# A four-layer graph network on one core: new first and last batches, relu of centred rows on ScalarE, identity transposes where TensorE would rest

## The chip, the cores and the metric

The kernel runs on one core of a Trainium2 chip. The metric is the device time of one execution in microseconds, median of several runs. A core has TensorE (PE, matmuls into eight PSUM banks), VectorE (DVE), ScalarE (ACT), GpSimd (POOL) and SyncE (SP, which issues DMA). All data is fp32, except two masks in bf16.

## The reference

Thirty-two graphs (batches) of 512 nodes with 128 features go through four layers. All share one sparse, symmetric adjacency matrix of 512 x 512. Each layer adds its result to x; before each, x is normalized over features and passed through relu.

```python
h = relu(layernorm(x)); x = x + gcn(h)        # layer 0
# A_hat = adj + I; d = rowsum(A_hat) ** -0.5
# gcn(h) = (d[:, None] * A_hat * d[None, :]) @ h @ W.T + b
h = relu(layernorm(x)); x = x + ggnn(h)       # layer 1, five steps:
# m = adj @ h
# z = sigmoid([m, m] @ w3.T + h @ u3.T + ...);  r = sigmoid([m, m] @ w4.T + h @ u3.T + ...)
# hv = tanh([m, m] @ w5.T + (r * h) @ u5.T + ...);  h = (1 - z) * h + z * hv
h = relu(layernorm(x)); x = x + elu(gat(h))   # layer 2
h = relu(layernorm(x)); x = x + gat(h)        # layer 3
# gat: g = h @ W; e = leaky_relu(src[:, None] + dst[None, :]); masked softmax over neighbours; @ g
```

The exponential of a leaky relu of a sum is a maximum of two products, so the kernel takes exponentials of three columns only, a maximum, and a product with the mask.

## The kernel before

Every operation is recorded with an engine, an estimated cost and a due time. A small list scheduler (`Plan`) simulates the engines and emits the instructions in the order it finds; it tries several parameter pairs and keeps the one with the earliest simulated end. Buffers (`bank` are the eight PSUM banks) are handed out by the plan too. On the chip each engine runs its own list in order and waits for semaphores.

Batches go in pairs. Two batches share the seven block products of a Strassen-like scheme (`products`, line L516 in the profile); batches 0 to 3 use plain products in layer 0 (`product`, L551):

```python
def product(h, mT, due):                              # L551
    p, m = Val("bank"), Val("m")
    for c in range(C):                                # C = 4, MM = 0.858
        op("PE", MM, due, lambda c=c: nc.tensor.matmul(flat(p.t), chunk(h, c), mT.t[:, c, :], start=(c == 0), stop=(c == C - 1)),
           r=[h[c], mT[c]], w=[p, m])
    op("ACT", A, due, lambda: nc.scalar.copy(flat(m.t), flat(p.t)), r=[p], w=[m])
    return m
```

At the start the adjacency is loaded, turned on TensorE (L285) and summed on VectorE (L288). GpSimd makes d by a power, TensorE spreads d over a row (L300), and VectorE makes the normalized matrix anT (L308, L311), which the first product of layer 0 needs. Weights are turned on TensorE (L364). The masks of layers 2 and 3 are made soon after (L340).

A gate step of layer 1 is three groups of matmuls (L603 to L618), three tanh and four VectorE operations. Its new state must be turned for the next step. This is done by DMA ("shuttle"), except in the last steps, where TensorE turns it (L448):

```python
if due >= STEPS * B - EASE:                           # EASE = 0
    p = to_features(new, due + 2, *([] if last else [h]))   # 4 transposes on TensorE
    [...]
```

The attention of the last four batches (`near`) does everything without DMA, since nothing is left to hide it:

```python
def norm(b, y, due):
    # norm_stats: 4 bn_stats (L406), 4 bn_aggr (L410), ve = var + eps (L411), rstd = ve ** -0.5 on GpSimd (L413)
    mv, rstd = norm_stats(b, due)
    for c in range(C):                                # L432
        op("DVE", 0.16, due, lambda c=c: nc.vector.tensor_scalar(
            y.t[:, c, :], xb.t[:, c, :], mv.t[:, c, 0:1], rstd.t[:, c:c + 1], op0=ALU.subtract, op1=ALU.mult), ...)
[...]
if near:
    norm(b, y, due)
    pT = to_features(y, due + 1, gT)                  # L448
    op("ACT", A, due + 1, lambda: nc.scalar.activation(gT..., pT..., AF.Relu), r=[pT], w=[gT])   # L663
[...]                                                 # heads: 4 matmuls of gT with w_aug (L678)
    # exp of three columns of each half (L680); g scaled by one of them (L685)
    spread()                                          # 4 transposes of a column into a bank (L698)
    op("ACT", A, due + 2, lambda: nc.scalar.copy(row..., pr...), r=[pr], w=[row, e])             # L700
for j in range(C):                                    # L713
    op("DVE", 0.68, due + 3, lambda j=j: nc.vector.scalar_tensor_tensor(
        e.t[:, j, :], row.t, h.t[:, j, D + 1:D + 2], maskT[l].t[:, j, :], op0=ALU.max, op1=ALU.mult), ...)
[...]                                                 # mix: 16 matmuls of e with g (L722; L733 for other batches)
```

Then come a reciprocal (L736), for layer 2 the product, exponential and elu (L738, L748 to L752), for layer 3 the last sum (L744) and the output DMA (L755). The near chain of a pass is thus: statistics, power, norm, turn, relu, heads, exponentials, spread, copy, e, mix, finish.

Of the kernel before, what the change touches and what calls it, by code (L numbers as in the profile page):

```python
# [15 lines left out]
P = 128  # L16
EPS = 1e-5
STEPS = 5
# [4 lines left out]
EASE = 0  # L23
FAR0, FAR1 = 2, 4
LANES = 6
# [13 lines left out]
class Op:  # L39
    def __init__(self, engine, cost, due, emit, delay):  # L40
        self.engine, self.cost, self.due, self.emit, self.delay = engine, cost, due, emit, delay
        self.waits, self.then, self.vals = 0, [], []


class Plan:
# [5 lines left out]
    def __init__(self, buffers, ends):  # L51
        self.buffers, self.ends, self.ops = buffers, ends, []

# [41 lines left out]
    def attempt(self, uses, last, hurry):  # L95
# [15 lines left out]
        now, count = 0.0, 0  # L111
# [6 lines left out]
        def start(e):  # L118
            if busy[e]:
                return  # L120
            kept = []
            while ready[e]:
# [4 lines left out]
                if not short:  # L127
                    for v in opens:
                        v.t = free[v.kind].pop()
                    busy[e] = True  # L130
                    o.at = now
                    order.append(o)
                    post(now + o.cost, 0, o)
                    post(now + o.cost + o.delay, 1, o)
                    break
                kept.append(key)
            for key in kept:
                heapq.heappush(ready[e], key)

# [9 lines left out]
        while events:  # L149
            now, _, kind, o = heapq.heappop(events)  # L150
            if kind == 0:
                busy[o.engine] = False
                settle(o, True)
            else:
                done += 1
# [12 lines left out]
def gnn_stack(ctx: ExitStack, tc: tile.TileContext, a: dict, out: bass.AP):  # L168
# [48 lines left out]
    }, [(last, hurry) for last in (170, 173, 176, 179) for hurry in (0.06, 0.08, 0.1, 0.12)])  # L217
# [15 lines left out]
    def load(name, shape, src, due, queue="SP", cost=0.45, delay=2.4):  # L233
# [7 lines left out]
    warm = fixed([P, 1], "warm")  # L241
    op("POOL", 0.8, -1000, lambda: make_identity(nc, ident.t), w=[ident])
    op("POOL", 0.1, -999, lambda: nc.gpsimd.memset(mhalf.t, -0.5), w=[mhalf])
    op("DVE", 0.1, -1000, lambda: nc.vector.memset(warm.t, 0.0), w=[warm])
    op("ACT", 1.4, -1000, lambda: nc.scalar.activation(warm.t, warm.t, AF.Tanh), w=[warm])

    adj_sb = Val("e", C)
    for c in range(C):
        e, q = (("SP", nc.sync), ("ACT", nc.scalar))[c % 2]
        op(e, 0.45, -1001, lambda c=c, q=q: q.dma_start(adj_sb.t[:, c, :], adj[c * P:(c + 1) * P, :]),  # L250
           w=[adj_sb[c]], delay=3.6)
    xs = []
    for b in range(B):
        v = Val("x", C)
        op("SP", 0.95, max(-995 + b, STEPS * b - 20) if b >= 8 else -995 + b, lambda v=v, b=b: nc.sync.dma_start(v.t, x[b].rearrange("(c p) d -> p c d", p=P)),
           w=[v], delay=3)
        xs.append(v)
    w0 = load("w0", [P, D], a["L0_gnn_W"], -993.5)
# [10 lines left out]
    for l, w in ((2, "L2_gnn_W"), (3, "L3_gnn_w")):  # L269
        w_aug[l] = fixed([P, D + 3], f"w_aug{l}", 2)  # L270
        op("SP", 0.45, -990.5, lambda l=l, w=w: nc.sync.dma_start(w_aug[l].t[:, :D], a[w]), w=[w_aug[l][0]], delay=2.4)
# [7 lines left out]
    deg, dinv = fixed(SMALL, "deg", C), fixed(SMALL, "dinv")  # L279
    for c in range(C):  # L280
        p = Val("bank")

        def turn_adj(c=c, p=p):
# [4 lines left out]
        op("DVE", 0.66, -801, lambda c=c: nc.vector.reduce_sum(deg.t[:, c:c + 1], adj_sb.t[:, c, :], axis=mybir.AxisListType.X),  # L288
           r=[adj_sb[c]], w=[deg[c]])
    op("DVE", 0.1, -799, lambda: nc.vector.tensor_scalar_add(deg.t, deg.t, 1.0), w=[deg])  # L290
    op("POOL", 1.0, -1000, lambda: nc.gpsimd.tensor_tensor(dinv.t, deg.t, mhalf.t, ALU.pow), r=[deg, mhalf], w=[dinv])


    anT = fixed([P, C, N], "anT", C)
    drow = Val("bank")
    dinv2 = fixed(SMALL, "dinv2")

    def turn_dinv():
        for c in range(C):
            nc.tensor.transpose(drow.t[:, c, :], dinv.t[:, c:c + 1].to_broadcast([P, P]), ident.t)  # L300
    op("PE", C * TURN, -798, turn_dinv, r=[dinv, ident], w=[drow])
    op("DVE", 0.1, -798, lambda: nc.vector.tensor_mul(dinv2.t, dinv.t, dinv.t), r=[dinv], w=[dinv2])
# [3 lines left out]

    for m in range(C):
        op("DVE", 0.7, -797, lambda m=m: nc.vector.scalar_tensor_tensor(  # L308
            anT.t[:, m, :], adjT.t[:, m, :], dinv.t[:, m:m + 1], flat(drow.t), op0=ALU.mult, op1=ALU.mult),
           r=[adjT, dinv, drow], w=[anT[m]])  # L310
        op("DVE", 0.26, -797, lambda m=m: nc.vector.scalar_tensor_tensor(  # L311
            block(anT.t, m), ident.t, dinv2.t[:, m:m + 1], block(anT.t, m), op0=ALU.mult, op1=ALU.add),
           r=[ident, dinv2], w=[anT[m]])
# [15 lines left out]
    of_adj, of_an = right_factors(adjT, -3), right_factors(anT, 5)  # L329


    maskT = {l: fixed([P, Q, N], f"maskT{l}", C, dtype=BF16) for l in (2, 3)}
    for l in (2, 3):
        far = Val(None, C)
        far.t = tiles(1, [Q, W, C, N], f"far_mask{l}", dram, BF16)[0]
        for c in range(C):
            part = Val("mask", 1)

            def edges(l=l, c=c, part=part):
                nc.vector.tensor_scalar(part.t, adjT.t[:, c, :], 0.0, None, op0=ALU.is_gt)  # L340
                if l == 2:
                    nc.vector.scalar_tensor_tensor(part.t[:, c * P:(c + 1) * P], block(adjT.t, c), -1.0, ident.t,
                                                   op0=ALU.mult, op1=ALU.is_lt)
            op("DVE", 0.35 if l == 3 else 0.6, 4 + l, edges, r=[adjT, ident], w=[part])
            op("SP", 0.4, 4 + l, lambda c=c, far=far, part=part: nc.sync.dma_start(
                far.t[:, :, c, :].rearrange("q i n -> (q i) n"), part.t), r=[part], w=[far[c]], delay=2.2)
        for c in range(C):
            op("SP", 0.4, 4 + l, lambda l=l, c=c, far=far: nc.sync.dma_start(
                maskT[l].t[c * W:(c + 1) * W], far.t[:, :, c, :].rearrange("q i n -> i q n")),
               r=[far], w=[maskT[l][c]], delay=2.2)  # L350
# [6 lines left out]
    def transposed(due, *group):  # L357
# [3 lines left out]
        for i, (parts, _) in enumerate(group):  # L361
# [3 lines left out]
            op("PE", len(parts) * MM1, due, turns, r=[ident, minus] + [q[0] for q in parts], w=[p[i]])  # L365
# [13 lines left out]
    w0T = transposed(-750, (one(w0), 1))  # L379
    gates = transposed(-700, (halves("w4"), 1), (one(raw["u3"]), 1), (halves("w3") + halves("w4", minus), 1), (halves("w5"), 1))  # L380
    u5T = transposed(-690, (one(raw["u5"]), 0.5))
    gats = transposed(-10, (one(w_aug[2]), 1), (one(w_aug[3]), 1))
# [9 lines left out]
    for i, l in enumerate((2, 3)):  # L392
        p = Val("bank")
        op("PE", 0.3, -9, lambda i=i, l=l, p=p: nc.tensor.matmul(p.t[:, 0, :2], gats.t[:, i, :], a_pair[l].t, start=True, stop=True),
# [5 lines left out]
        op("DVE", 0.3, -9, columns, r=[p], w=[w_aug[l][1]])  # L400
# [15 lines left out]
    def norm_relu(b, y, due):  # L416

        xb, off = xs[b], Val("off")
        mv, rstd = norm_stats(b, due)
        op("DVE", 0.1, due, lambda: nc.vector.scalar_tensor_tensor(off.t, mv.t[:, :, 0], -1.0, rstd.t, op0=ALU.mult, op1=ALU.mult),  # L420
# [6 lines left out]
    def norm(b, y, due):  # L427
# [3 lines left out]
        for c in range(C):  # L431
            op("DVE", 0.16, due, lambda c=c: nc.vector.tensor_scalar(  # L432
                y.t[:, c, :], xb.t[:, c, :], mv.t[:, c, 0:1], rstd.t[:, c:c + 1], op0=ALU.subtract, op1=ALU.mult),
               r=[xb[c], mv, rstd], w=[y[c]])

# [111 lines left out]
    def product(h, mT, due):  # L547

        p, m = Val("bank"), Val("m")
        for c in range(C):  # L550
            op("PE", MM, due, lambda c=c: nc.tensor.matmul(flat(p.t), chunk(h, c), mT.t[:, c, :], start=(c == 0), stop=(c == C - 1)),  # L551
               r=[h[c], mT[c]], w=[p, m])
        op("ACT", A, due, lambda: nc.scalar.copy(flat(m.t), flat(p.t)), r=[p], w=[m])
        return m


# [239 lines left out]
```

The softmax here doesn't subtract the row's maximum and nothing guards it: scores larger than these inputs give would overflow.

## Time and profile before

| | us |
|---|---|
| median of 3 runs (1642.45 to 1643.86) | 1642.52 |
| span of the profiled execution | 1643.0 |
| TensorE busy (7250 instructions) | 1617.2 |
| VectorE busy | 1378.8 |
| ScalarE busy | 715.6 |
| GpSimd busy | 144.0 |
| DMA: 159.80 MB, mean | 97 GB/s |

How to read the profile: busy time is the union of an engine's instructions. The profile counts every fp32 matmul as two records and a transpose as one. The ends of matmuls are modelled and overlap, so the distance from one start to the next says more than a duration. The chain goes back from the last instruction: at each step to what released it, or to the instruction before it on its engine. A wait line reads "engine, line <- engine, line that released it: us in total, times, longest".

### The profile page before, as it was taken

The page shows a single profiled execution, that of the slowest core. Times are in us where ns is not written, and L with a number is a line of the kernel's source. Part 1 is how long each engine was busy: PE and PEld are TensorE (multiplying, and loading weights), DVE is VectorE, ACT ScalarE, POOL GpSimd, SP SyncE. Part 2 cuts the span into 40 slices and gives each one's busy share as a digit, 9 for nine tenths or more (in the row PEclk, how much of TensorE's full clock was granted, in tenths as well). Part 3 has the DMA queues.
Part 4 walks back from the last instruction along what each step waited for, and adds up shares of the span by engine and source line. Part 5 has one row for each costly group of instructions (what it writes and reads, how often), then busy time and mean ns, then how long its engine had stood idle before and what let it go on. Part 6 is the DMA issues. An engine that isn't in the chain of part 4 may idle for free.

```text
span 1643.0 us, 23716 instructions
## 1 busy us (share of the span) xinstructions
PE 1617.2 (98%) x7250; PEld 1163.2 (71%) x7250; DVE 1378.8 (84%) x3937; ACT 715.6 (44%) x1573; POOL 144.0 (9%) x136
## 2 busy tenths in 40 slices
PE   8999999999999999999999999999999999999997
PEld 5666567776776777776776767767767777766787
DVE  7977588988888898888888888898887888787897
ACT  4643353535345353343535245343443535343442
POOL 2200000010001111010101001111000000000100
PEclk9999999999999999999999999999999999999999
DMA  5433253543435344353443535344363433424100
GB/s 148 110 74 72 54 123 97 122 103 100 113 84 142 79 110 101 91 141 93 110 113 84 129 90 134 98 105 107 87 139 75 104 76 83 126 72 110 39 27 26
DMA packets 380639, 159.80 MB, mean 97 GB/s; under 512 B 206080, under 2 KB 362080, under 8 KB 380512
## 3 DMA queue, kind: packets, MB, share of 16 engines
q1 hardware_dynamic: 380224, 157.77, 39.3%
q8 instruction: 57, 0.93, 0.2%
q14 instruction: 70, 0.57, 0.1%
q10 hardware_dynamic: 288, 0.52, 0.1%
HBM read 87.30 MB, written 70.89 MB: 96 GB/s over the span
## 4 chain that ended last, share of the span: by engine, by line
PE 94%; DVE 4%; DMA 1%; SPq 0%; issue 0%; ACT 0%; DVEq 0%
PE bank L516 33%; PE bank L733 12%; PE bank L617 8%; PE bank L618 8%; PE bank L610 8%; PE bank L603 8%; PE bank L604 8%; PE bank L678 3%; PE bank L722 2%; PE bank L572 1%; DVE st L406 1%; PE bank L448 1%; DVE S L504 0%; DVE m L529 0%; DMA e<-in_adj_dram 0%
## 5 line engine op out<-in xcount | busy, mean ns | idle before, releaser
L516 PE MATMUL bank<-made,S 128*128 128x256 f32 x1128 | 273.2, 380 | 4.1 <-DVE m L529 3.2
L413 POOL TENSOR_TENSOR rstd<-ve,mhalf 128x4 f32<-128x4 f32 x128 | 142.2, 1113 | 1469.8 <-DVE ve L411 1209.0
L516 PEld LDWEIGHTS bank<-made,S 128*128 128x128 f32 x1128 | 217.2, 196 | 43.3 <-issue 15.6
L521 ACT COPY half<-bank 128x256 f32<-128x256 f32 x282 | 104.7, 371 | 261.9 <-PE bank L516 257.7
L733 PEld LDWEIGHTS bank<-h_gat,e 128*128 128x128 f32 x1792 | 207.3, 192 | 12.8 <-issue 10.0
L733 PE MATMUL bank<-h_gat,e 128*128 128x129 f32 x1792 | 208.5, 275 | 0.2 <-DVE e L713 0.2
L606 ACT ACTIVATE r<-bank,gate_bw 128x512 f32<-128x512 f32 x160 | 109.5, 684 | 196.7 <-PE bank L604 180.2
L622 DVE TENSOR_TENSOR hv<-hv,hT 128x512 f32<-128x512 f32 x160 | 109.7, 686 | 87.4 <-ACT hv L620 86.6
L713 DVE SCALAR_TENSOR_TENSOR e<-row,h_gat,maskT 128x512 f32<-128x512 f32 x256 | 182.7, 741 | 0.0
L608 DVE SCALAR_TENSOR_TENSOR rh<-r,hT 128x512 f32<-128x512 f32 x160 | 109.8, 686 | 77.1 <-ACT r L606 74.3
L617 PE MATMUL bank<-m,wT 128*128 128x512 f32 x320 | 163.5, 592 | 0.0
L603 PE MATMUL bank<-m,wT 128*128 128x512 f32 x320 | 163.4, 592 | 0.0
L618 PE MATMUL bank<-rh,wT 128*128 128x512 f32 x320 | 163.4, 592 | 0.0
L604 PE MATMUL bank<-hT,wT 128*128 128x512 f32 x320 | 163.4, 592 | 0.0
L610 PE MATMUL bank<-m,wT 128*128 128x512 f32 x320 | 163.2, 592 | 0.0
L620 ACT ACTIVATE hv<-bank,gate_bw 128x512 f32<-128x512 f32 x160 | 109.6, 685 | 118.5 <-PE bank L618 117.0
L516 PE MATMUL bank<-adjT,h 128*128 128x256 f32 x640 | 160.6, 380 | 0.4 <-ACT h L423 0.3
L516 PEld LDWEIGHTS bank<-adjT,h 128*128 128x128 f32 x640 | 122.7, 196 | 26.4 <-issue 14.1
L529 DVE TENSOR_TENSOR m<-half,bank 128x256 f32<-128x256 f32 x282 | 115.6, 411 | 25.7 <-PE bank L516 13.7
L612 ACT ACTIVATE z<-bank,gate_bw 128x512 f32<-128x512 f32 x160 | 109.4, 685 | 58.7 <-PE bank L610 54.5
L406 DVE BATCH_NORM_STATS2 st<-x 128x6 f32<-128x128 f32 x512 | 122.4, 277 | 3.6 <-DMA x<-in_x_dram 3.3
L618 PEld LDWEIGHTS bank<-rh,wT 128*128 128x128 f32 x320 | 60.8, 190 | 76.5 <-issue 67.2
(115 smaller groups left out, 2218.2 us busy)
## 6 DMA issues: line engine op xcount, KB each, us to landing
far<-sq SPq DMA_DIRECT2D x936, 64.0 KB
h<-far SPq DMA_DIRECT2D x248, 128.0 KB
gT<-far SPq DMA_DIRECT2D x56, 256.0 KB
row<-line SPq DMA_DIRECT2D x56, 256.0 KB
x<-in_x_dram SPq DMA_DIRECT2D x32, 256.0 KB
out_dram<-x SPq DMA_DIRECT2D x32, 256.0 KB
h<-far SPq DMA_DIRECT2D x28, 256.0 KB
hT<-far SPq DMA_DIRECT2D x104, 64.0 KB
```

What stands on the lines that cost most here:

```text
L406: op("DVE", 0.21, due, lambda c=c: nc.vector.bn_stats(st.t[:, c, :], xb.t[:, c, :]), r=[xb[c]], w=[st[c]])
L413: op("POOL", 1.0, due, lambda: nc.gpsimd.tensor_tensor(rstd.t, ve.t, mhalf.t, ALU.pow), r=[ve, mhalf], w=[rstd])
L516: nc.tensor.matmul(low(r), u[:, l, :], factors[k][0]()[:, l, :], start=fresh and l == 0, stop=l == 1, skip_group_check=not fresh)
L529: op("DVE", HV, due - 5, lambda: nc.vector.tensor_add(out(), u.t, low(t)), r=[u, t], w=[o])
L603: nc.tensor.matmul(flat(gate.t), gates.t[:, 0, :], flat(m.t), start=True, stop=False)
L604: nc.tensor.matmul(flat(gate.t), gates.t[:, 1, :], flat(hT.t), start=False, stop=True)
L608: op("DVE", V, due - 5, lambda: nc.vector.scalar_tensor_tensor(flat(rh.t), flat(r.t), 1.0, flat(hT.t), op0=ALU.add, op1=ALU.mult), r=[r, h ...
L610: op("PE", MM, due + 0.3, lambda: nc.tensor.matmul(flat(gate.t), gates.t[:, 2, :], flat(m.t), start=False, stop=True, skip_group_check=Tru ...
L617: nc.tensor.matmul(flat(cand.t), gates.t[:, 3, :], flat(m.t), start=True, stop=False)
L618: nc.tensor.matmul(flat(cand.t), u5T.t[:, 0, :], flat(rh.t), start=False, stop=True)
L713: op("DVE", 0.68, due + 3, lambda j=j: nc.vector.scalar_tensor_tensor(e.t[:, j, :], row.t, h.t[:, j, D + 1:D + 2], maskT[l].t[:, j, :], op ...
L733: nc.tensor.matmul(pt()[:, c, :D + 1], e.t[:, j, i * P:(i + 1) * P], h.t[:, j, :D + 1], start=(j == 0), stop=(j == C - 1))
```

## The change

It leaves the middle of the computation as it is and redoes both ends:

- *Start.* x of batch 0 is loaded before the adjacency. TensorE runs eight matmuls on a cleared tile while nothing has landed. Layer 0 of batches 0 to 3 multiplies with adjT itself (and a small tile for the blocks on the diagonal with the identity added); d is put into the normalized input and into the last sum instead. So the first product needs neither anT nor the spread of d; these are made after the second product. Two of the four degree sums go to ScalarE. The masks are made later. `begin(b + 2)` records layer 0 of the next pair before layer 1 of this one.
- *Early steps.* The state of the steps with due below 8 (four of them) is turned on TensorE.
- *Near attention.* Since relu(r * (x - mean)) = r * relu(x - mean) for positive r, ScalarE makes relu(x - mean) at once. r goes into the exponentials as a scale and into one small product. The row is read by VectorE from PSUM and not copied; masks in the order this needs are put into anT's memory, which is free by then. Elu and output go in halves.
- *Where the plan leaves TensorE idle.* From 1420 us of the plan's time, if TensorE has rested 0.9 us of the last 3.4 of that time, the plan adds a transpose of the identity into a free bank. Nobody reads it. It is there to hold TensorE's clock.
- Other parameter pairs for the plan.

The core of the diff, with cuts marked `[...]`:

```diff
-EASE = 0
+EARLY = 8
+IDLE_FROM = 1420
+RUN_UP = 8
[...]
+        def keep_going():
+            since = now - self.SPAN                          # 3.4
[...]
+            rest = self.SPAN - sum(min(b, now) - max(a, since) for a, b in work if a < now)
+            if rest < self.REST:                             # 0.9
[...]
+            v = Val("bank")
+            v.t, v.uses = free["bank"].pop(0), 1
+            o = Op("PE", self.IDLE, 0, lambda: self.idle(v), 0)
[...]
-    }, [(last, hurry) for last in (170, 173, 176, 179) for hurry in (0.06, 0.08, 0.1, 0.12)])
+    }, [(171, 0.05), (173, 0.04), (175, 0.07), (176, 0.1), (179, 0.14)],
+        IDLE_FROM, lambda v: nc.tensor.transpose(v.t[:, 0, :], ident.t, ident.t))
[...]
+    def turn_nothing():
+        for _ in range(RUN_UP):
+            nc.tensor.matmul(run_up.t[:, 0, :], warm.t[:, 0, :], warm.t[:, 0, :], start=True, stop=True)
+    op("PE", 0.43 * RUN_UP, -1002, turn_nothing, r=[warm], w=[run_up])
[...]
+        if c < 2:
+            op("ACT", 0.7, -801, lambda c=c, junk=junk: nc.scalar.activation(
+                flat(junk.t), adj_sb.t[:, c, :], AF.Copy, accum_out=deg.t[:, c:c + 1]), ...)
[...]
+    def center_relu(b, y, due):
+        for a in range(2):
[...]                                          # bn_stats and bn_aggr of two row blocks, off = -mean
+            for c in (2 * a, 2 * a + 1):
+                op("ACT", 0.385, due, lambda c=c: nc.scalar.activation(
+                    y.t[:, c, :], xb.t[:, c, :], AF.Relu, bias=off.t[:, c:c + 1]), r=[xb[c], off[a]], w=[y[c]])
+        op("DVE", 0.1, due, lambda: nc.vector.tensor_scalar_add(ve.t, mv.t[:, :, 1], EPS), r=[mv], w=[ve])
+        op("POOL", 1.0, due, lambda: nc.gpsimd.tensor_tensor(rstd.t, ve.t, mhalf.t, ALU.pow), r=[ve, mhalf], w=[rstd])
[...]
-    def product(h, mT, due):
+    def product(h, due):
[...]
+            def times(c=c):
+                for lo, hi in ((0, c), (c, c + 1), (c + 1, C)):
+                    if lo < hi:
+                        right = diag.t[:, c, :] if lo == c else adjT.t[:, c, lo * P:hi * P]
+                        nc.tensor.matmul(flat(p.t)[:, lo * P:hi * P], h.t[:, c, :], right, ...)
[...]
-        if due >= STEPS * B - EASE:
+        if not EARLY <= due < STEPS * B:
[...]
         if near:
-            norm(b, y, due)
+            rstd, g = center_relu(b, y, due), Val("off", 2)
             pT = to_features(y, due + 1, gT)
-            op("ACT", A, due + 1, lambda: nc.scalar.activation(... AF.Relu), r=[pT], w=[gT])
+            op("ACT", A, due + 1, lambda: nc.scalar.copy(flat(gT.t), flat(pT.t)), r=[pT], w=[gT])
[...]
+                    for c in range(2):
+                        nc.scalar.activation(ht()[:, c, D:D + 3], qt()[:, c, D:D + 3], AF.Exp,
+                                             scale=rstd.t[:, 2 * a + c:2 * a + c + 1])
+                op("DVE", 0.08, due + 1, lambda a=a, ht=ht: nc.vector.tensor_mul(
+                    g.t[:, 2 * a:2 * a + 2], ht()[:, :, D], rstd.t[:, 2 * a:2 * a + 2]), ...)
[...]
-            op("ACT", A, due + 2, lambda: nc.scalar.copy(row..., pr...), r=[pr], w=[row, e])
+            row, rows, masked, mask = pr, flat, kept[0], lambda j: kept[1](l, j)
```

## The prediction, made before the changed kernel ran

> **What bounds the kernel now.** I read the page first: the busy time of each engine, the slices and the chain that ended last.
>
> ```profile
> PE 1617.2 (98%) x7250; PEld 1163.2 (71%) x7250; DVE 1378.8 (84%) x3937; ACT 715.6 (44%) x1573; POOL 144.0 (9%) x136
> PE   8999999999999999999999999999999999999997
> PE 94%; DVE 4%; DMA 1%; SPq 0%; issue 0%; ACT 0%; DVEq 0%
> ```
>
> TensorE is busy in 98% of the span and holds 94% of the chain. Nothing outside TensorE can give much, except where it waits. So I made a ledger of the span: the work that TensorE must do, and the rest. For the work I need the distance from one matmul to the next, not its duration (these overlap). The chain in order of time gives it, from runs of one kind:
>
> ```profile
> 201.28 8.63 PE bank L516 x40
> 248.63 3.57 PE bank L733 x32
> 1585.70 0.86 PE bank L610 x2
> 1586.56 0.44 PE bank L448 x4
> ```
>
> The columns are start, length, and what. So a record with 256 columns takes 8.63/40 = 0.216 us, one with 129 takes 0.112, one with 512 takes 0.43, one transpose 0.11. (Each fp32 matmul is two records, each transpose one.) The groups kept apart by shape count 2632 records of 256 columns, 1632 of 512, 2048 of 129, 512 of 131, and 422 of 128 with the transposes: 2632 x 0.216 + 1632 x 0.429 + 2560 x 0.112 + 422 x 0.111 = 568 + 700 + 287 + 47 = 1602 us. The span is 1643.0. TensorE's first record starts at 5.0 us and its last ends at 1638.0, 5.0 before the end. That leaves 1643 - 1602 - 10 = 31 us in which TensorE waits or is slow. The table by stage says where:
>
> ```profile
> 0.00:15.00 15.00, 8.46 (x44) 7.82 (x45) 7.60 (x28) 6.55 (x14) 2.79 (x9) 1.00 0.76 210
> 15.00:50.00 35.00, 33.74 (x121) 19.62 (x120) 33.55 (x146) 21.22 (x50) 9.77 (x9) 1.00 0.45 126
> 50.00:100.00 50.00, 48.94 (x193) 34.88 (x192) 44.97 (x165) 24.22 (x55) 9.70 (x9) 1.00 0.43 91
> 100.00:1450.00 1350.00, 1346.88 (x5906) 963.09 (x5905) 1136.76 (x3165) 590.18 (x1278) 106.97 (x96) 1.00 0.42 101
> 1450.00:1586.50 136.50, 134.09 (x634) 94.84 (x633) 110.40 (x292) 54.96 (x124) 8.75 (x8) 1.00 0.27 69
> 1586.50:1612.00 25.50, 24.57 (x213) 23.61 (x212) 25.00 (x81) 9.72 (x27) 3.50 (x3) 1.00 0.04 11
> 1612.00:1630.00 18.00, 13.10 (x87) 12.19 (x85) 12.75 (x48) 8.07 (x24) 2.52 (x2) 0.81 0.05 16
> 1630.00:1643.00 13.00, 7.38 (x64) 7.22 (x64) 7.72 (x20) 0.67 (x3) 0.00 (x0) 0.97 0.21 61
> ```
>
> The columns are the stage, its length, then busy time of PE, PEld, DVE, ACT and POOL, the granted clock, and DMA. In the 1350 us of the middle TensorE is idle for 3.1 us. In the first 100 it is idle for 6.5 + 1.3 + 1.1 = 8.9, of which 5.0 are the landing of the adjacency. From 1586.5, just after the last gate matmul, it is idle for 0.9 + 4.9 + 5.6 = 11.4, and the clock falls to 0.81 in one stage. The change can only win at the two ends. The chain of the end shows the second one:
>
> ```profile
> 1617.97 0.17 DVE ve L411
> ...
> 1618.53 0.76 DVE e L713
> 1619.29 0.04 issue
> 1619.33 3.81 PE bank L722 x16
> 1623.14 1.71 PE bank L448 x8
> ```
>
> Sixteen L722 records cost 3.81 us there, against 16 x 0.112 = 1.79 elsewhere; eight transposes 1.71 against 0.88. TensorE stood still for 3.2 us before it (the waits list "PE bank L722 <- DVE e L713: 4.3, 2, 3.2"), and ran at half speed after.
>
> **What the Trainium skill says.** "TensorE: Matmul & The Clock Gate", Part 1, says that the array runs at half rate until it has been busy for a window of about 3.4 us, and falls back after an idle one. The trace agrees: at the start 16 transposes took 3.65 us (0.228 each, twice 0.11), and the end is as above. Part 4 of that page says that a transpose does not count as busy in the same way; nothing in the trace before settles this, and it is the doubtful point of the change's identity transposes. "ScalarE: Activation LUTs", What ACT_TABLE_LOAD costs, says that each [128,1] operand of an activation adds about 93 ns. The trace has 482 ns for the relu with bias and scale, so my estimate for the new one with bias alone is 390 ns. "VectorE: DVE Perf Modes", The TRN2 errata, gives an operation that reads PSUM a larger fixed cost than one that reads SBUF (120 against 58 cycles). The trace does not show it: anT<-adjT,dinv,bank reads PSUM and takes 741 ns, e<-row,h_gat,maskT reads SBUF and takes 744. So I take 0.74 us for the new e too.
>
> **The change, part by part.**
>
> *TensorE's own work.* I counted matmuls in the order of instructions of both kernels. Four steps of the first pair (due below 8) now turn their state on TensorE instead of by DMA: 16 transposes x 0.11 = +1.8 us. The products of batches 0 to 3 are cut into 40 matmuls instead of 16, with the same columns: by the fixed part of about 3 ns in each distance above, +0.2. The 29 identity transposes (3.2 us) and the 8 warm-up matmuls (16 records) lie where TensorE has nothing else. Sum: **+2 us**.
>
> *The start.* Before, the first product starts at 14.1 us. By the work ahead of it (16 transposes, 22 weight records and 4 transposes of dinv: 42 x 0.11 = 4.6) it could start at 5.0 + 4.6 = 9.6. The 4.5 us between are the cold clock (16 x 0.12 = 1.9 on the transposes, about 1.2 on the first ten weight records) and the wait of 1.6 for anT. After: the warm-up matmuls begin at about 1.2 us on a cleared tile, so the clock should rise at 5 to 8 instead of about 10: saves 1.5 to 2. The first product reads adjT and a diagonal tile and no longer needs anT nor dinv's transposes: saves 1.6 + 0.4. It needs the scaled y of batch 0, whose chain is the degrees (2 on ScalarE, 2 on VectorE, 0.7 each), the power (1.0) and four multiplies (0.25 each): adjacency at about 5 + 1.5 + 0.2 + 1.1 + 0.4 for the first piece, near 8.5, earlier than the weights, which come by DMA to about 10. Against it, x of batch 0 is loaded ahead of the adjacency: 256 KB more before it, at the stage's 210 GB/s up to +1 us, in part hidden. Between 15 and 100 TensorE waits 2.3 us (copies of m, L516 behind L529, VectorE 96% busy from 15 to 50). Moving the masks, anT and half of the degrees off VectorE's first 50 us should give back some 1.5. Sum: -1.8 - 2.0 - 1.5 + 0.3 = **-5 us**.
>
> *The end, one near pass* (norm, turn, heads, row, e, mix). Before, the chain holds ve 0.17, the power on GpSimd 1.0 and four norms 1.1 between the statistics and the transposes. After, the relu follows the means of each half directly, 4 x 0.29 + 0.1 = 1.3 us on ScalarE (step of 0.385 less 0.093), and the power goes beside the transposes and heads: -1.0. The row is no longer copied from PSUM: -0.59 and a hand-over, together -0.65. More exponentials (four instead of two) and the small multiply for g (0.15): +0.2. So -1.45 a pass, and layers 2 and 3 of the last pair follow each other: -2.9. Elu and output in halves let statistics start on the first half: about -0.7. If the clock stays up: -(3.81 - 1.79) - (1.71 - 0.88) = -2.8, less 0.4 for identity transposes in the way of real work. VectorE: five of the passes lie after 1586.5 (20 norms of L432); each loses 4 x 0.256 and gains 4 small operations of 0.08, -0.7, so -3.5 in all of 45.5 busy us; that shortens queues, and I take -1 of it as path. Sum: **-7 us**.
>
> *The middle.* The scheduler orders all anew with other parameters. Before, it leaves 3.1 + 2.4 us idle from 100 to 1586; I take no change, with a spread of 3.
>
> Total: 1642.5 + 2 - 5 - 7 = **1632.5 us**.
>
> **Rivals.**
> 1. *Identity transposes do not hold the clock*, or come at the wrong moment since the plan's clock is not the chip's. For it: the skill's Part 4. Against: at the start (in the timeline) the ten weight records from 8.4 us take 0.24 each and those from 10.6 on 0.11, so the clock rose 5.6 us after the first transpose and only 2.2 after the first plain matmul. Then the 2.8 stay: 1635.
> 2. *VectorE becomes the bound of the end.* It is 25.0 of 25.5 us busy from 1586.5 to 1612. Then only its own saving of 3.5 counts: 1636. Against: from 1612 on it is idle for 10.5 of 31 us, mostly behind TensorE ("DVE rden L736 <- PE bank L722: 7.0, 4, 4.9").
> 3. *Banks.* e now reads its row from PSUM, so a bank is held for four e (4 x 0.66 us) instead of one copy of 0.59. With eight banks the heads or mixes of another batch may wait: 1 or 2 us a pass, 1636 to 1639.
> 4. *The middle gets worse.* Each missed hand-over of L516 costs about 0.6 us (seen singly before); ten more would give 1638, and a stall of a load nearer 1645.
> 5. *The start is held by loads.* If weights still arrive at 11 or 12, it gains 2 and not 5: 1635.5.
>
> **Range and chances.** The rivals cost 3 to 6 each and hardly all come together: above, 1640. Below: if both ends give all that is idle there (31 us, of which some 12 can't go: the middle, the landing of the mixes), 1624. Range **1624 to 1640**. Faster by over 2% would need 1609.7, which is 33 us, more than all waits of TensorE together: chance **0.01**. Slower by over 2% needs a stall of 33 us that is not there now: **0.01**. Within 2%: **0.98**.
>
> **What would show it.** TensorE should count about 7359 records (7250 + 48 + 16 + 29 + 16), the first product should start near 10.5 to 11 us, the 16 first transposes should take nearer 2.5 than 3.65 us, the clock should be 1.00 in every stage of the end, no power should stand in the end's chain, and the time from the last gate matmul to the end should be near 49 instead of 56.5 us. I am wrong if the start still waits for loads, if the clock falls in the end all the same, if a wait for a bank (matmuls behind e) appears, or if the stretch from 100 to 1450 has more than 6 us of idle TensorE.

## The result, and the profile after

| | before | changed |
|---|---|---|
| median, us (6 runs each) | 1642.61 (1641.45 to 1643.95) | 1633.05 (1632.89 to 1633.99) |
| span of the profiled execution | 1643.0 | 1632.2 |
| TensorE records | 7250 | 7359 |

The ratio is 0.9941, 95% interval 0.9929 to 0.9954: 9.6 us less.

First the page of the changed kernel: busy time, TensorE's 40 slices, the chain by engine.

```profile
PE 1618.1 (99%) x7359; PEld 1170.1 (72%) x7359; DVE 1383.1 (85%) x3973; ACT 726.6 (45%) x1625; POOL 143.4 (9%) x136
PE   9999999999999999999999999999999999999998
PE 96%; DVE 2%; ACT 1%; DMA 1%; POOL 0%; issue 0%; DVEq 0%; POOLq 0%; ACTq 0%
```

The first digit of the slices was 8 and the last 7: both ends are fuller, and VectorE's share of the chain fell from 4% to 2%. The table by stage of the changed kernel (stage, its length, busy time of PE, PEld, DVE, ACT, POOL, granted clock, DMA share, GB/s):

```profile
0.00:15.00 15.00, 11.65 (x74) 10.38 (x74) 9.11 (x49) 6.64 (x16) 4.68 (x10) 1.00 0.75 210
15.00:50.00 35.00, 34.54 (x178) 26.26 (x177) 34.21 (x142) 22.13 (x52) 8.97 (x8) 1.00 0.31 77
50.00:100.00 50.00, 50.00 (x190) 34.08 (x189) 39.28 (x147) 24.87 (x56) 10.71 (x9) 1.00 0.15 32
100.00:1450.00 1350.00, 1348.08 (x5917) 964.48 (x5916) 1150.66 (x3195) 592.37 (x1287) 105.23 (x96) 1.00 0.42 104
1450.00:1581.00 131.00, 128.98 (x619) 91.86 (x618) 107.63 (x291) 56.31 (x135) 8.77 (x8) 1.00 0.26 70
1581.00:1605.00 24.00, 22.47 (x196) 21.68 (x195) 20.25 (x74) 14.37 (x48) 2.99 (x3) 1.00 0.04 12
1605.00:1620.00 15.00, 14.55 (x125) 13.74 (x125) 14.79 (x56) 8.23 (x30) 2.01 (x2) 1.00 0.07 19
1620.00:1632.30 12.30, 7.79 (x70) 7.60 (x69) 7.15 (x25) 1.72 (x8) 0.00 (x0) 0.99 0.23 65
```

The last gate matmul ends at 1581.2 (before: 1586.4). The end after it has lost its hole: the 15 us from 1605 have 14.55 of busy TensorE at clock 1.00, where before the 18 us from 1612 had 13.10 at 0.81. (The 0.99 of the last stage falls behind TensorE's last record.)

Busy time flatters TensorE, because identity transposes and slow matmuls count in it. So I keep the prediction's ledger for every run: from each stretch I subtract the work, its records times the distance from one to the next (0.429, 0.3235, 0.216, 0.112 and 0.1095 us for 512, 384, 256, about 129 columns and a transpose), without run-up and identity transposes. What is left is *loss*. It is taken from one profiled execution of each kernel.

| us | 0-15 | 15-100 | 100-1450 | 1450 to last gate | after it | sum of loss | work |
|---|---|---|---|---|---|---|---|
| before | 9.5 | 4.3 | 5.6 | 4.5 | 16.4 | 40.3 | 1602.6 |
| changed | 7.3 | 1.1 | 3.7 | 4.7 | 10.8 | 27.5 | 1604.7 |
| difference | -2.2 | -3.3 | -2.0 | +0.2 | -5.6 | -12.8 | +2.1 |

-12.8 + 2.1 = -10.7, the difference of the two spans (that of the medians is 9.6). Of the 12.8 us of loss that went, 5.6 are in the end, 5.5 in the first 100 us and 2.0 in the middle.

How the end closed is seen in its chain (start, length, what), which runs through VectorE from layer 2 of the last two batches to the matmuls that follow:

```profile
1604.36 2.73 DVE e L829 x4
1607.08 0.67 DVE v L869 x2
1607.75 0.67 DVE x L871 x2
1608.42 0.78 DVE st L470 x4
...
1610.98 0.69 DVE v L869 x2
1611.67 0.67 DVE x L871 x2
1612.34 0.78 DVE st L470 x4
1613.12 0.16 DVE mv L474 x2
1613.30 0.17 DVE off L475
...
1613.89 0.66 DVE e L829
...
1614.60 2.05 PE bank L838 x16
```

VectorE handles the two last batches one after the other: elu and statistics of one (1607.08 to 1609.9), then of the other (1610.98 to 1613.9). The first one's relu, turn and heads run on ScalarE and TensorE meanwhile, so its e is the next thing VectorE does and TensorE waits 0.3 us. Each pair of bn_aggr is followed by a negation that depends on it and has its whole 0.17 in the chain.

### The profile page after: what moved, and what is told of

Same layout as the page of the kernel before. It is cut to its first block, busy times and chain, and to the rows that moved or that the text cites. A ratio compares the mean times of both kernels' runs of the same rounds, so it can differ in the third digit from the quotient of the medians.

```text
span 1632.2 us, 24002 instructions
## 1 busy us (share of the span) xinstructions
PE 1618.1 (99%) x7359; PEld 1170.1 (72%) x7359; DVE 1383.1 (85%) x3973; ACT 726.6 (45%) x1625; POOL 143.4 (9%) x136
## 4 chain that ended last, share of the span: by engine, by line
PE 96%; DVE 2%; ACT 1%; DMA 1%; POOL 0%; issue 0%; DVEq 0%; POOLq 0%; ACTq 0%
PE bank L564 35%; PE bank L849 12%; PE bank L697 8%; PE bank L698 8%; PE bank L711 8%; PE bank L704 8%; PE bank L712 8%; PE bank L787 3%; PE bank L656 2%; PE bank L838 1%; PE bank L603 1%; PE bank L496 1%; DVE e L829 1%; POOL rstd L439 0%; DMA e<-in_adj_dram 0%; DMA w<-in_L_gnn_w_w_dram 0%
## 5 line engine op out<-in xcount | busy, mean ns | idle before, releaser
L564 PE MATMUL bank<-made,S 128*128 128x256 f32 x1128 | 269.5, 380 | 1.2 <-ACT half L569 0.9
L439 POOL TENSOR_TENSOR rstd<-ve,mhalf 128x4 f32<-128x4 f32 x120 | 133.0, 1109 | 1397.4 <-DVE ve L437 1145.9
L829 DVE SCALAR_TENSOR_TENSOR e<-row,h_gat,maskT 128x512 f32<-128x512 f32 x224 | 161.3, 740 | 0.0
L432 DVE BATCH_NORM_STATS2 st<-x 128x6 f32<-128x128 f32 x480 | 115.4, 279 | 5.5 <-DMA x<-in_x_dram 5.2
L698 PEld LDWEIGHTS bank<-hT,wT 128*128 128x128 f32 x320 | 60.8, 190 | 76.5 <-issue 75.8
```

Source lines behind the costliest of these rows:

```text
L432: op("DVE", 0.21, due, lambda c=c: nc.vector.bn_stats(st.t[:, c, :], xb.t[:, c, :]), r=[xb[c]], w=[st[c]])
L439: op("POOL", 1.0, due, lambda: nc.gpsimd.tensor_tensor(rstd.t, ve.t, mhalf.t, ALU.pow), r=[ve, mhalf], w=[rstd])
L564: nc.tensor.matmul(low(r), u[:, l, :], factors[k][0]()[:, l, :], start=fresh and l == 0, stop=l == 1, skip_group_check=not fresh)
L698: nc.tensor.matmul(flat(gate.t), gates.t[:, 1, :], flat(hT.t), start=False, stop=True)
```

## The experiments

Each kernel was timed beside the kernel before; ratios are to it. "After" means the changed kernel. Each kernel's plan makes its own order, and some choose another of the parameter pairs, so an edit can move more than its own lines: the changed kernel and runs 4, 10, 11 and 12 take (171, 0.05), runs 3 and 9 (173, 0.04); the kernel before takes (176, 0.1), run 5 (179, 0.12), run 6 (176, 0.08), run 7 (176, 0.1). Only runs 1, 2 and 8 keep an order fixed and omit instructions; every other figure below is that of an edit together with the order that the plan makes for it. Two parts of the change, elu and output in halves and the new parameter pairs, have no run of their own.

**1. Identity transposes left out, order kept.**

```diff
-            o = Op("PE", self.IDLE, 0, lambda: self.idle(v), 0)
+            o = Op("PE", self.IDLE, 0, lambda: None, 0)
```

> The changed kernel with its plan and its order unchanged, only the 29 identity transposes are not emitted. Theory A (the transposes hold TensorE's clock in the end, as the prediction had it): the clock falls for at least one window in the end, the stretch from the last gate matmul to the end grows from 50.8 to about 53 us, total about 1635.5. Theory B (the waits of the new order are too short to let it fall, the transposes do nothing): clock 1.00 to the end, total 1632.5 to 1633.3.

Measured: 1633.27 us (1632.78 to 1634.71), ratio 0.9942 (0.9928 to 0.9955). The record of the clock in its trace shows it never below full until TensorE's last record, with 29 records less. In the changed kernel the transposes have no effect that shows: real work is now dense enough.

**2. Run-up left out.** `for _ in range(RUN_UP)` became `range(0)`.

> The changed kernel with the same plan and order, only the eight warm-up matmuls are not emitted. Theory A (the cold clock stands in the path of the start): the 16 transposes of the adjacency take about 0.21 us each again, the first product starts at about 13 instead of 11.5 us, total 1634.5 to 1635. Theory B (the start is held by the loads of the weights and by the power for dinv, not by the clock): the first product still starts by 11.8 us, total 1633.

Measured: 1633.02 us (1632.76 to 1633.65), ratio 0.9938 (0.9926 to 0.9951): no loss either, as theory B said. In the profiled executions the clock rises at 10.3 us instead of 3.9, and the first product starts at 11.70 instead of 11.48. The timeline of TensorE in the changed kernel says why (start, busy, what; in brackets the idle time before it and what ended it):

```profile
5.10 0.63 PE L332 MATMUL bank<-ident,e 128*128 128x128 f32 x4 [0.64 <-DMA e<-in_adj_dram]
6.73 1.53 PE L332 MATMUL bank<-ident,e 128*128 128x128 f32 x12 [0.99 <-DMA e<-in_adj_dram]
...
9.14 1.16 PE L390 MATMUL bank<-ident,w 128*128 128x128 f32 x8 [0.67 <-DMA w<-in_L_gnn_w_w_dram]
...
11.48 0.39 PE L603 MATMUL bank<-v,y 128*128 128x128 f32 x2
```

With a warm clock the 16 transposes take 0.63 + 1.53 = 2.16 us instead of 3.65 before, and TensorE then waits for what still has to land: one part of the adjacency (0.99) and the gate weights (0.67). With a cold clock it fills those waits with slow work.

Nor does the run-up bring the clock surely. Run 3 starts with the same instructions, and its clock rises at 9.9 us and its first product starts at 12.12; in runs 1 and 9, also with the same start, the clock rises at 7.2 and the first product starts at 10.81 and 10.90. The loss of the first 15 us is 6.7 in both of these, 7.3 in the changed kernel with its clock at 3.9, 7.8 in run 3 and 7.4 here: an early clock is worth 1 us at most.

**3. Old norm in the near passes of after**: mean and r applied by VectorE, relu on the turned bank, one exponential per half.

```diff
-            rstd, g = center_relu(b, y, due), Val("off", 2)
+            norm(b, y, due)
-            op("ACT", A, due + 1, lambda: nc.scalar.copy(flat(gT.t), flat(pT.t)), r=[pT], w=[gT])
+            op("ACT", A, due + 1, lambda: nc.scalar.activation(flat(gT.t), flat(pT.t), AF.Relu), r=[pT], w=[gT])
[...]    # exponentials without scale, two columns of heads times the plain exponential
```

> The changed kernel with the near attention's old norm: statistics, power, four norms on VectorE, relu at the copy out of PSUM, no scale in the exponentials; the row is still read from PSUM. Latency theory (the prediction): each of the two passes in sequence is 1.0 us longer because the power and the norms stand before the turn, total about 1635, with the power in the chain of the end. Work theory (VectorE's and TensorE's throughput bound the end, the power is hidden): the chain shows VectorE back to back and no power; five passes after the last gate put back 4 x 0.256 and take away about 0.5, total 1634.5 to 1636. If neither binds: 1633.

Measured: 1638.06 us (1637.59 to 1638.53), ratio 0.9968 (0.9956 to 0.9981): 5.0 of the 9.6 are gone. Loss after the last gate is 16.1 instead of 10.8, and VectorE is busy for 48.9 us there instead of 42.2. Its chain of the end:

```profile
1606.48 1.02 POOL rstd L439
...
1610.30 1.34 DVE v L864 x4
1611.64 1.34 DVE x L866 x4
1612.98 1.55 DVE st L432 x8
...
1616.83 2.05 DVE y L460 x8
1618.88 0.67 DVE e L824
...
1619.60 1.16 PE bank L833 x8
```

The power is on the chain again, as the latency theory said, but the total is above what either theory gave. The larger part is what follows: both batches reach elu, statistics and norm together, and VectorE spends 9.25 us (1610.30 to 1619.55) before TensorE's next mix can start. Between 1612 and 1625 the loss, with identity transposes counted in it, is 5.3 us there and 1.3 in after.

VectorE's 6.7 us more after the last gate are not all the norm's. By count, 30 of the multiplications e lie there instead of 24: the plan moved six that belong before the last gate, 0.66 us each, 3.9 in all. The edit itself accounts for about 2.8.

**4. Work for VectorE alone**: after, plus four scratch operations of 128 columns in each near pass, which nobody reads.

```diff
+        pad = Val("rh", C)
+        for c in range(C):
+            op("DVE", 0.16, due, lambda c=c: nc.vector.tensor_scalar(
+                pad.t[:, c, :], xb.t[:, c, :], mv.t[:, c, 0:1], mv.t[:, c, 1:2], op0=ALU.subtract, op1=ALU.mult), ...)
```

> The changed kernel, with four operations of 128x128 added on VectorE to every near pass (the old norms' size and number, into a scratch tile that nobody reads): VectorE's work of the old norm without its place in the chain. Work theory (VectorE's throughput bounds the end): five passes after the last gate x 4 x 0.256 = 5.1 us more, total 1637 to 1638.5. Latency theory (the old norm cost 5 us because power and norms stand before the turn): 1632.7 to 1634.

Measured: 1635.15 us (1634.75 to 1636.67), ratio 0.9953 (0.9941 to 0.9966). VectorE has 47.0 - 42.2 = 4.8 us more in the end, with the same operations beside the padding, and the total is 2.1 more (1.7 to 3.6 in its executions): 0.44 for each, between the two theories. At that price the 2.8 us which the old norm itself adds would be 1.2 of the 5.0 of run 3, and 2.9 with the six moved e. The rest would go with the power, the norm's place in the chain and the other order; these were not separated, as run 3 takes another parameter pair.

**5. Centred relu put into the kernel before**, alone: row copy, masks, elu, start and parameters as before. (Its values differ, as the expectations of runs 5 and 7 say: in the kernel before the nodes are put into the order of the masks after the turn, while r stays in the order of the rows, so a node is scaled by another node's r. The change has both in one order. Instructions and shapes are the same, so this bears on the values and not on the time. It holds for runs 5, 7 and 8.)

```diff
-            norm(b, y, due)
+            rstd, g = center_relu(b, y, due), Val("off", 2)
[...]    # exponentials with scale r, heads times g, as in the change
```

> The kernel before with the relu of centred rows alone: the near passes make relu(x - mean) on ScalarE, the scale goes into the exponentials and into g; row copy, masks, elu and start as before (the scale meets the nodes in another order than they are turned in, so values differ from the reference's; the work is the same). Work theory: VectorE loses about 5 us after the last gate, total 1637 to 1639. If the end of the kernel before is held by the slow clock and by waits of TensorE rather than by VectorE: 1641 to 1643.

Measured: 1640.93 us (1638.02 to 1642.52, 13 runs), ratio 0.9984 (0.9976 to 0.9993): 1.9, where undoing it cost 5.0. Its 13 runs differ by the granted clock: four with 0.999 or 1.000 took 1638.0 to 1638.8, eight with 0.997 or 0.998 took 1640.4 to 1642.5, one with 0.999 took 1640.9. In the profiled one the clock is at half between 1618.2 and 1621.6. The same instructions on the same chip, 3 us apart: that looked like the price of the clock, which the next three runs test. An estimate from these numbers: 3.4 us at half clock cost at most 1.7, so they do not make up the whole 2.2 to 2.9 by which the profiled execution is behind the first group; a mean of 0.997 stands for some 10 us at half clock (2 x 0.003 x 1640), which could.

**6. Identity transposes put into the kernel before**, alone (55 of them).

> The kernel before, with the rule for identity transposes (from 1420 us of the plan's time, 0.9 us of rest in 3.4) and nothing else of the change. Theory A (they hold the clock): clock 1.00 in the end, total 1639.5 to 1640.5, a gain of 2 to 3 us. Theory B (transposes do not count as work for the clock): it falls all the same, total 1642 to 1643. If they stand in the way of real matmuls: slower than before by up to 1 us.

Measured: 1643.32 us (1642.57 to 1644.52, 13 runs), ratio 1.0001 (0.9993 to 1.0009), granted clock 0.999 or 1.000 in all 13 runs; the kernel before beside it had 0.998 in 16 of 17. They hold the clock, and the kernel with them, in an order of its own, gains nothing. Loss after the last gate falls from 16.4 to 14.7, between 1450 and the gate it rises from 4.5 to 6.2.

**7. Centred relu and identity transposes in the kernel before.**

> The kernel before with the centred relu of the near passes and with the rule for identity transposes, nothing else (its values differ from the reference as in the run with the relu alone, because the exponents' scale comes later; the work is the same). Theory A (the clock is what the relu alone left in the end: its runs at full clock were near 1638.5, the others near 1641): clock 0.999 to 1.000 in every run, and all runs near 1638 to 1639.5. Theory B (the identity transposes cost by their place what they give, as they did when added alone to the kernel before): clock 1.000, but 1640 to 1642.

Measured: 1643.33 us (1642.48 to 1644.24, 13 runs), ratio 1.0002 (0.9993 to 1.001), clock 1.000 in 12 runs and 0.999 in one. Both theories had the clock, but neither the time: it is slower than with the relu alone. The plan made another order, from another of its parameter pairs, as the stretch from the last gate matmul to the end shows: 55.0 us here, 47.9 with the relu alone. That order too has a hole in which TensorE waits for others (before, 3.2 us; with the relu alone, 2.0), and here the transposes fill it (chain of this kernel):

```profile
1612.89 0.63 ACT r L812
1613.52 0.50 ACT gT L719
...
1616.31 2.75 PE bank L253 x25
1619.07 1.99 PE bank L504 x8
```

L253 is the identity transpose: 25 in a row, 2.75 us in which TensorE has no work.

**8. The order of run 7, transposes left out**, by the same edit as in run 1.

> The kernel before with centred relu and identity-transpose rule, in exactly that order, but the identity transposes are not emitted (about 60 records less; values as in the runs with the relu). It tells the clock from the order: the run with the relu alone and the one with relu and transposes have different orders of work in the end. Theory A (the clock is worth something when the order is held fixed): the clock falls near 1617 to 1620 where 25 transposes stood, the matmuls after it run at half speed, 1645 to 1646.5. Theory B (the transposes are in the way as much as they hold the clock, and the order made the difference): clock at 0.998 or so, but 1642.5 to 1644.

Measured: 1644.28 us (1643.57 to 1645.8, 13 runs), ratio 1.0008 (1.0 to 1.0017). With the order held fixed, 62 transposes are worth 0.95 us on the medians, between the two theories. The stages from 1590 to 1625 of this kernel, the clock in the third column from the right:

```profile
1590.00:1610.00 20.00, 16.95 (x138) 16.63 (x137) 16.93 (x66) 12.34 (x42) 3.22 (x3) 0.91 0.05 14
1610.00:1625.00 15.00, 11.65 (x78) 9.62 (x77) 13.47 (x49) 7.12 (x21) 2.91 (x2) 0.90 0.06 18
```

and with the transposes (run 7):

```profile
1590.00:1610.00 20.00, 18.37 (x164) 17.96 (x163) 18.24 (x68) 12.36 (x42) 3.22 (x3) 1.00 0.05 14
1610.00:1625.00 15.00, 14.43 (x119) 13.03 (x118) 11.82 (x49) 9.76 (x33) 2.91 (x2) 1.00 0.07 20
```

The clock does fall twice without them: 8 matmuls of L734 take 2.08 us in its chain, with them 1.09. In the profiled execution, the slowest of the thirteen, loss after the last gate is 17.9 against 15.7; the gap of the medians is half of that. The thirteen fall into two groups as in run 5: eight with 0.999 took 1643.6 to 1644.7, five with 0.997 or 0.998 took 1645.2 to 1645.8. So holding the clock is worth about 1 us here at the median, and some 2 against the executions in which it is lost most. Whether the 3 us between the groups of run 5 are all of this kind is not shown.

**9. Row copied by ScalarE again**, in after.

```diff
-            op("PE", C * TURN, due + 2, spread, r=[*exps, ident], w=[pr, e])
-            row, rows, masked, mask = pr, flat, kept[0], lambda j: kept[1](l, j)
+            op("PE", C * TURN, due + 2, spread, r=[*exps, ident], w=[pr, row])
+            op("ACT", A, due + 2, lambda: nc.scalar.copy(row.t, flat(pr.t)), r=[pr], w=[row, e])
+            masked, mask = kept[0], lambda j: kept[1](l, j)
```

> The changed kernel, with the row copied from PSUM to SBUF by ScalarE again before VectorE reads it. The prediction's step (0.65 us a pass, two passes in sequence): 1634.3. Work theory (VectorE's work is the same, ScalarE has room): 1632.7 to 1633.5. If a bank held for four e was in the way: below 1632.5.

Measured: 1636.61 us (1636.36 to 1637.18), ratio 0.996 (0.9947 to 0.9972): +3.6, more than any of the three expectations, and in the order of another parameter pair. TensorE's waits in its end (waiting line, what it waits for: us in total, times, longest):

```profile
PE bank L839 <- DVE e L830: 1.8, 3, 1.4
...
PE bank L255 <- ACT row L818: 0.6, 1, 0.6
```

and in after:

```profile
PE bank L838 <- DVE x L860: 0.8, 1, 0.8
...
PE bank L838 <- DVE e L829: 0.3, 1, 0.3
```

The copy stands between the turn and e, and on ScalarE between heads of the other batch; its chain has 0.80 of exponentials and 0.48 of copy ahead of one e.

**10. Four early turns by DMA again** (EARLY = 0, in after).

> The changed kernel with the four early steps turned by DMA again (16 transposes fewer, 1.8 us of TensorE's work). If the early turns pay: TensorE waits for h in the first 60 us, total 1634 to 1637. If the work of other batches hides the DMA there as before: 1631 to 1631.7.

Measured: 1633.66 us (1633.29 to 1633.79), ratio 0.9941 (0.9929 to 0.9953). The work falls by 1.8, the loss of the first 100 us rises by 0.8 and that between 1450 and the last gate by 1.2: the turns on TensorE give what they cost, or 0.6 more (the executions of the two kernels overlap).

**11. First products by the normalized matrix again**, made before them (after otherwise: loads, run-up, degrees, late masks and the end stay).

```diff
-        ms = [product(y, due + i) for i, y in enumerate(ys)] if first else products(*ys, factors["an"], due + 1)
+        ms = [product(y, factors["anT"], due + i) for i, y in enumerate(ys)] if first else products(*ys, factors["an"], due + 1)
[...]    # anT at -797 as before; no diagonal tile; no d in the relu or in the sum
```

> The changed kernel, but the products of batches 0 to 3 read the normalized adjacency again, made before them, and no diagonal tile; run-up, order of loads, degrees, masks and the whole end stay as changed. Theory A (the prediction's start: not waiting for anT and the turns of dinv is worth 2.0, and VectorE's relief in the first 50 us more): first product at 13 to 14.5 instead of 11.5, loss of the first 100 us 10.5 to 12 instead of 8.4, total 1635 to 1637. Theory B (the start is held by the landing of weights and by the power of the degrees, which stay): first product at 12 or so, total 1633 to 1634.

Measured: 1634.67 us (1634.0 to 1635.27), ratio 0.995 (0.9937 to 0.9962): +1.6. First product at 13.13. Its waits of TensorE up to 60 us:

```profile
PE bank L594 <- DVE anT L616: 1.5, 1, 1.5
...
PE bank L385 <- DMA w<-in_L_gnn_w_w_dram: 0.8, 1, 0.8
```

The wait for anT is back with nearly its old length (1.6), as theory A said of the first product; the total lies between the two theories. Loss by stage: 8.2 from 0 to 15 (after 7.3), 0.9 from 15 to 100 (after 1.1), 4.5 from 100 to 1450 (after 3.7). So the fall of the loss from 15 to 100, 4.3 to 1, does not come from the diagonal form.

**12. An attempt to beat the change**: v of the near passes of layer 2 by ScalarE, meant to take 2.5 us off VectorE in the end.

```diff
-                op("DVE", 0.335, due + 4, lambda some=some, pt=pt: nc.vector.tensor_mul(v..., pt()..., rden...), ...)
+                def mean(a=a, pt=pt):
+                    for c in range(2):
+                        nc.scalar.mul(v.t[:, 2 * a + c, :], pt()[:, c, :D], rden.t[:, 2 * a + c:2 * a + c + 1])
+                op("ACT", 2 * 0.385, due + 4, mean, r=[p, rden[a]], w=[v[a]])
```

> The changed kernel, but in the near passes of layer 2 the mix times 1/denominator is made by ScalarE (two of 128 columns, 0.37 each) instead of VectorE (one of 256 columns, 0.41). Theory A (VectorE's work is half of the end: 4.8 us of padding cost 2.1, so 0.44 of each us): 6 of them at 0.41 lie in the end, 2.5 x 0.44 = -1.1, so 1631.5 to 1632.5. Theory B (the place in the chain counts: +0.33 a half, and another hand-over, twice in the last pair): 1633 to 1634.5.

Measured: 1636.32 us (1635.97 to 1638.28), ratio 0.9963 (0.995 to 0.9975): +3.3, worse than either theory. Chain of its end:

```profile
1604.46 2.73 DVE e L829 x4
1607.19 1.34 DVE v L875 x4
1608.53 1.34 DVE x L877 x4
1609.87 1.56 DVE st L470 x8
...
1613.19 1.31 DVE e L829 x2
...
1615.95 0.38 PE bank L255
```

The two batches, which after kept apart by a whole elu and set of statistics, fall into step again: v x4, x x4, st x8 in one block, and the next e follows 6 us after the block began. In the profiled run the clock is at half from 1616.1 to 1619.5. But VectorE was not relieved: it is busy for 42.2 us after the last gate, as in after. The six v (2.1 us) are gone from there, but more of the e of other batches lie behind the last gate than in after (1.5), and small operations that no longer follow one another closely take 1.0 more. So the run shows what another order can cost, and not what a lighter VectorE would give. No run beat the changed kernel by more than the spread.

## Why the prediction held, step by step

It said 1632.5; it is 1633.05. The sum held better than its terms: the end gave 1.4 less than foretold and the middle gave 2.0 that were not foretold. That the total is within 0.6 us is luck.

- **TensorE's work, +2**: +2.1, and 7359 records, as counted.
- **The start, -5**: -5.5, but by two wrong sizes that cancel. Up to 15 us the cold clock (-1.5 to -2), anT (-2.0) and x first (+0.3) should have given 3 to 4; they gave 2.2, and the first product came at 11.48 instead of 10.5 to 11. The term that failed is the clock: leaving out the run-up costs 0 (run 2). (The three parts of the 4.5 us ahead of the first product, 1.9, 1.2 and 1.6, add up to 4.7, and 256 KB at 210 GB/s are 1.2 us and not 1; neither decides anything.) Rival 5 was half right: TensorE runs into landings at once (0.99 and 0.67). The term of anT is worth 1.6 as a whole (run 11). The stretch from 15 to 100 was sized -1.5 and is -3.3; TensorE idles for 0.5 us there instead of 2.3. The reason given for it, less work for VectorE in the first 50 us, is not what the tables show: VectorE is busy for 9.11 + 34.21 = 43.3 us there instead of 7.60 + 33.55 = 41.2, and only from 50 to 100 for less (39.28 instead of 44.97). Of TensorE's 2.3 us of waits before, 1.7 ended with ScalarE (0.9 for copies of m, 0.5 for half, 0.3 for h) and 0.6 with VectorE. Which of late masks, degrees on ScalarE, the order of loads and the new order of the plan brings the gain was not separated; the diagonal form does not.
- **The middle, 0 within 3**: -2.0. It idles 1.9 us instead of 3.1. The loss is 4.5 when the first products are made the old way (run 11), 3.7 and 3.2 in runs 1 and 2, which keep the order of the changed kernel. The gain lies in the new order and was not traced.
- **The end, -7**: -5.6, from last gate to end 51.0 us, not 49. Its terms are off in both directions. *The row*: 0.65 a pass, 1.3 in all; undoing it costs 3.6. *Power, norm and VectorE's load*: -1.6 and -1; undoing costs 5.0. *The clock*, -2.8 + 0.4: it is full up to TensorE's last record, as foretold, but run 1 has that without the transposes and without any loss. So the step "identity transposes hold the clock, and that saves 2.8" failed: the slow clock of before (half from 1618.3 to 1625.1) went with the hole that had let it fall, and how much of the 5.6 this is was not separated. Where a hole is open (run 8) the transposes gave 0.95. The undone parts sum to 8.6, more than the end gained, so they overlap. That each reopens the same hole would explain it, but is not shown: runs 3 and 9 also change the order.
- **Small operations**: four of 0.08 a pass were meant. The groups of the changed kernel from 1581 on (busy, mean ns, idle before and its releasers) give the price:

```profile
L478 ACT ACTIVATE y<-x,off 128x128 f32<-128x128 f32 x20 | 6.7, 396 | 5.6 <-DVE off L475 5.6
L829 DVE SCALAR_TENSOR_TENSOR e<-bank,h_gat,anT 128x512 f32<-128x512 f32 x24 | 16.9, 744 | 0.1
L792 ACT ACTIVATE h_gat<-bank,rstd 128x3 f32<-128x3 f32 x24 | 4.7, 261 | 4.3 <-PE bank L787 4.2
L475 DVE TENSOR_SCALAR off<-mv 128x2 f32<-128x2 f32 x10 | 1.7, 170 | 0.4
```

The relu with bias takes 396 ns (estimate 390), e from PSUM 744 (0.74, the same as from SBUF). But the negation after the means takes 0.17 in the chain, twice a pass, since it depends on the operation before it; and two exponentials with a scale, of 3 columns, take 261 ns each against 176 for the one of 6 columns before. Means and negations of a pass cost 4 x 0.08 + 2 x 0.17 + hand-overs = 0.70 in the chain, the old ones 0.30 + 0.17.
- **Rivals.** 1: wrong in its mechanism, since identity transposes do hold the clock (runs 7 and 8), and without effect here. 2: VectorE is not the bound, but near: 42.2 us busy in the end, where 45.5 - 3.5 = 42 was foretold, and each us more costs 0.44 (run 4); from 1605 to 1620 it is busy for 14.79 of 15 us, and the chain runs through it. 3: the held bank does not show; matmuls wait 0.3 us behind e, and with the copy 1.8. 4: the middle improved.
- **No power in the end's chain**: true, but no proof, as the chain before lists none after 1586 either. There the prediction had the path wrong: it counted 1.0 a pass for a power that it took to be in the chain. Run 3 shows the power in the chain (1606.48) only where the old norm is put back into the changed kernel.

## What to carry to other kernels

In an end where several engines hand on short pieces, do not count a saving by its own length: undoing the centred relu cost 5.0 and undoing the free row 3.6, more together than the end had gained, and the relu alone in the kernel before gave 1.9. Part of these figures is the order that the plan made each time. Look whether two streams that share an engine go in step or apart: in runs 3 and 12 they fell into step, and the kernel was 5.0 and 3.3 us slower. Keep the order fixed when one instruction's effect is to be measured in a kernel whose plan reorders, and compare what lies in a stretch before comparing its busy time.

## What was not expected of the hardware

- Identity transposes keep TensorE's clock up where it has no other work: 0.999 to 1.000 in 26 of 26 executions with them (runs 6 and 7), 0.997 to 0.999 in 13 of 13 with the order of run 7 and without them. The Trainium skill, "TensorE: Matmul & The Clock Gate", Part 4, says that a transpose does not count as busy in the same way; with these fp32 transposes the measurement is otherwise. They raise the clock too: in run 7 TensorE turns the adjacency from 4.91 to 8.35 us, 0.21 us a transpose and nothing else, and after only 0.6 us of other matmuls the records of these are 0.11 apart instead of 0.23.
- Eight matmuls from 1.05 us on did not fix when the clock rises: 3.9, 7.2, 7.2 and 9.9 us in the changed kernel and runs 1, 9 and 3, which start with the same instructions.
- One kernel, one chip, two groups of times by granted clock: 1638.0 to 1638.8 and 1640.4 to 1642.5 (run 5). Run 8 has two such groups. What tips it was not found.
- VectorE operations of 2 to 4 columns last 0.15 to 0.17 us. In the end of the changed kernel one that does not depend on the one before it starts 0.07 to 0.09 us after it; the negation, which needs the bn_aggr just before it, starts 0.18 after it (once 0.25).
